# A recommender with neighbour attention on one core: the final part in program order, buffers outside the item stage's space, the last rows finished at once, indices loaded first

## The chip, the core and the metric

The kernel runs on one core of a Trainium2 chip. The metric is device microseconds of one execution. TensorE is called PE, VectorE DVE, ScalarE ACT, GpSimd POOL and SyncE SP, as in the profile.

## What is computed

```python
def neighbour_attention(E, near):                 # 50,001 items, 32 neighbours each
    V = E[near]
    w = softmax(einsum('nd,nkd->nk', E, V) / sqrt(32))
    return einsum('nk,nkd->nd', w, V)
a_sus, a_inf = neighbour_attention(E_in, near), neighbour_attention(E_out, near)
h = concat(E_hist[history], a_sus[history], a_inf[history])    # 128 wide
t = concat(E_tgt[target], a_inf[target], a_sus[target])
z = relu((h * t) @ W1.T + b1)                                  # 128 hidden units
score = z @ W2[0]                                              # one per history entry
```

There are 16384 users with 100 history entries and one target each. The scores of a user go through an exponential, entries equal to the target or to item 0 drop out, and the weighted rows are compared with the target row; a norm over all users enters into the last step, after which a sigmoid gives one number per user.

## The kernel before, in words

**Item stage.** The 50,001 items lie in 23 tiles of 128 partitions x 17 items (`NITER`, `NSUB`). A sub-tile is one item per partition, and two sub-tiles are a batch (`M = 2`), so there are 391 sub-tiles in 196 batches; the last batch has one. `load` (L124 to L129, on SP) brings a tile's neighbour indices `nidx`, its own embeddings `own`, and the first 64 columns of its result `row`. `gather` (L144, on POOL) issues 64 indirect DMAs per batch, each of which fetches one neighbour row for 128 items. `products` multiplies them by the items' own rows (L157 on ACT, L159 on DVE), reduces to scores (L166), and takes the exponentials (L176, ACT). `attended` weights the rows and sums them (L192, L200) and writes the two attention results into `row` (L203). `finish` works once per tile: ACT copies 32 columns (L217), DVE makes the row sum in column 0 (L218), and ACT issues two writes into tables in DRAM: `ttab` (L219, the target's layout) and `table` (L222, 129 columns, for the history). For the last tile it works twice, on 16 rows and on the last one. In the loop over batches `gather(b)` comes first, then `attended(b - 2)`, `products(b - 1)` and `finish(b - 3)`. Engines take their instructions in the order of this code, with waits on semaphores between them; DVE, ACT and SP are in manual schedule here.

The first 64 columns of `ttab` are copied from the target embedding (L109, L110, 12.5 MB, issued by ACT before the loop). The weights `b1`, `w2`, `w1` are loaded on SP before the first tile (L86 to L90), and `w1T` and `pick` are set up from them (L93 to L99).

**User stage.** 128 columns of 128 users; a column has 25 steps of 4 history entries. Per column there is one gather of target rows (L270) and then four gathers of history rows per step (L306), all on POOL; `hidx` are the history indices (L266, SP, four columns a load), `tidx` the target's (L246). PE turns the rows (L320), DVE multiplies them by the turned target (`xT`, L325) and copies the row sums (`hsum`, L328), PE makes the hidden layer (L337), ACT the relu (L339), PE the scores into a bank (L345). `LAG = 3` steps lie between these. There are 20 buffers of rows (`HBUF`). At the end of a column ACT copies the bank (L351), PE turns it (L358), ACT takes exponentials (L360), and DVE sums (L367 to L370). `target_work` (L282 to L293) makes the turned target `tT`, its sum `tsum`, its sum of squares `tsq` (ACT, L288) and the mask `keep`.

**Final part.** `root` is the square root of `den` (L406), `part` and its sum follow on DVE, PE adds over partitions (L413), and DVE and ACT make the norm `n1`, the targets' norms `n2` from `tsq` (L422 the maximum, L423 the square root), `pred` and the sigmoid `res` (L430), which SP writes out (L431). Its tiles are in a pool `f_s` of its own, opened after the pools of the user stage are closed, and the part is not in manual schedule; where its instructions land in an engine's order is the scheduler's choice.

The pools decide who waits for whom beyond the data: `u_in` (history indices), `u_t`, `u_h` (row buffers) are opened after the item stage's pools are closed and take over their space.

Of the kernel before, what the change touches and what calls it, by code (L numbers as in the profile page):

```python
# [53 lines left out]
def kernel(  # L54
# [31 lines left out]
    nc.sync.dma_start(b1_sb, b1.rearrange("(h o) -> h o", o=1))  # L86
# [6 lines left out]
    nc.vector.memset(pick, 0.0)  # L93
    for g in range(NG):
        nc.vector.tensor_copy(pick[:, g, g : g + 1], w2_sb)
    with tc.tile_pool(name="wps", bufs=1, space=bass.MemoryType.PSUM) as wps:
        w1_ps = wps.tile([D, HID], F32, name="w1_ps")
        nc.tensor.transpose(w1_ps, w1_sb, ident)
        nc.vector.tensor_copy(w1T, w1_ps)  # L99


    scale = 1.0 / math.sqrt(G)
    near_v = near.rearrange("(i p j) k -> i p j k", p=P, j=NSUB)
# [6 lines left out]
    nc.scalar.dma_start(ttab[ITEMS - 1 : ITEMS, 0:DE], etgt[ITEMS - 1 : ITEMS, :])  # L110
    with (
        tc.manual_schedule(engines={E.Activation, E.DVE, E.SP}),
        tc.tile_pool(name="n_in", bufs=2) as n_in,
# [21 lines left out]
        def gather(b):  # L135
            v = n_v.tile([P, M, K, 2, G], F32, name="v")
            subs[b]["v"] = v
            for m, s in enumerate(subs[b]["tiles"]):
                it, j = divmod(s, NSUB)
                if j == NSUB // 2 and it + 1 < NITER:  # L140
                    load(it + 1)
                nidx = its[it][0]
                for k in range(K):
                    nc.gpsimd.indirect_dma_start(  # L144
                        out=v[:, m, k].rearrange("p t d -> p (t d)"),
                        out_offset=None,
                        in_=egeo,
                        in_offset=bass.IndirectOffsetOnAxis(ap=nidx[:, j, k : k + 1], axis=0),
                    )
# [60 lines left out]
        def finish(b):  # L210
            for s in subs.pop(b)["tiles"]:
                it, j = divmod(s, NSUB)
                row = its[it][2]
                if j == NSUB - 1 or (it == NITER - 1 and j == NSUB - 2):
                    j0 = NSUB - 1 if it == NITER - 1 and j == NSUB - 1 else 0
                    js = slice(j0, j + 1)
                    nc.scalar.copy(row[:, js, W : W + G], row[:, js, 1 + DE : 1 + DE + G])  # L217
                    nc.vector.tensor_reduce(row[:, js, 0], row[:, js, 1:W], AX.X, ALU.add)  # L218
                    nc.scalar.dma_start(  # L219
                        ttab_v[it][:, js, DE:D], row[:, js, 1 + DE + G : W + G]  # L220
                    )
                    nc.scalar.dma_start(table_v[it][:, js, :], row[:, js, 0:W])  # L222
                if j == NSUB - 1:
                    del its[it]
# [1 line left out]
        NT = NITER * NSUB  # L226
        batches = [range(s, min(s + M, NT)) for s in range(0, NT, M)]
        load(0)
        for b in range(len(batches) + 3):
            if b < len(batches):  # L230
                subs[b] = {"tiles": batches[b]}
                gather(b)
            if 0 <= b - 2 < len(batches):
# [6 lines left out]
    num = const.tile([P, UC], F32, name="num")  # L240
    den = const.tile([P, UC], F32, name="den")
    tsum = const.tile([P, UC], F32, name="tsum")
    tsq = const.tile([P, UC], F32, name="tsq")
    hist_v = history.rearrange("(p i j) l -> i p j l", p=P, j=BSUB)
    tidx = const.tile([P, UC], I32, name="tidx")
    nc.scalar.dma_start(tidx, target.rearrange("(p c) -> p c", p=P))  # L246
    tidf = const.tile([P, UC], F32, name="tidf")
    nc.vector.tensor_copy(tidf, tidx)
    with (
        tc.manual_schedule(engines={E.PE, E.Activation, E.DVE, E.SP, E.Pool}),  # L250
        tc.tile_pool(name="u_in", bufs=4) as u_in,
        tc.tile_pool(name="u_t", bufs=3) as u_t,
        tc.tile_pool(name="u_h", bufs=HBUF) as u_h,
        tc.tile_pool(name="u_x", bufs=6) as u_x,
        tc.tile_pool(name="u_z", bufs=6) as u_z,
        tc.tile_pool(name="u_s", bufs=3) as u_s,
# [4 lines left out]
        users, hists = {}, {}  # L261
        rows, got, hT, xT, z = {}, {}, {}, {}, {}

        def history_of(i):
            hists[i] = u_in.tile([P, BSUB, L], I32, name="hidx")
            nc.sync.dma_start(hists[i], hist_v[i])  # L266

        def target_rows(c):
            t = u_t.tile([P, D], F32, name="t")
# [100 lines left out]
            nc.vector.tensor_reduce(num[:, c : c + 1], ea, AX.X, ALU.add)  # L370

        last = UC * NG
        history_of(0)
        history_of(1)
        target_rows(0)
        target_work(0)
        for s in range(last + 2 * LAG + 6):
# [21 lines left out]
                ended(done)  # L399

    with (
        tc.tile_pool(name="f_s", bufs=1) as f_s,
        tc.tile_pool(name="f_p", bufs=1, space=bass.MemoryType.PSUM) as f_p,
    ):
        root = f_s.tile([P, UC], F32, name="root")
        nc.scalar.activation(root, den, AF.Sqrt)  # L406
        part = f_s.tile([P, UC], F32, name="part")
        nc.vector.reciprocal(root, root)
        nc.vector.tensor_tensor(part, num, root, ALU.mult)
        psum1 = f_s.tile([P, 1], F32, name="psum1")  # L410
# [3 lines left out]
        s = f_s.tile([P, 1], F32, name="s")  # L414
        nc.vector.tensor_copy(s, s_ps)
        n1 = f_s.tile([P, 1], F32, name="n1")

        nc.vector.tensor_tensor(n1, s, s, ALU.mult)
        nc.vector.tensor_scalar(n1, n1, float(D), EPS * EPS, ALU.mult, ALU.max)
        nc.scalar.activation(n1, n1, AF.Sqrt)  # L420
        n2 = f_s.tile([P, UC], F32, name="n2")
        nc.vector.tensor_scalar(n2, tsq, EPS * EPS, None, ALU.max)  # L422
        nc.scalar.activation(n2, n2, AF.Sqrt)  # L423
        nc.vector.tensor_scalar(n2, n2, n1, None, ALU.mult)
        pred = f_s.tile([P, UC], F32, name="pred")
        nc.vector.tensor_scalar(pred, tsum, s, None, ALU.mult)
        nc.vector.reciprocal(n2, n2)
        nc.vector.tensor_tensor(pred, pred, n2, ALU.mult)
        res = f_s.tile([P, UC], F32, name="res")
# [57 lines left out]
```

## Time and profile before

| | us |
|---|---|
| median of 3 runs | 36254.43 |
| these runs | 36249.81 to 36257.75 |
| the profiled execution's own time | 36158.99 |
| its span, first to last instruction | 36157.2 |
| item stage until the last gather's end | 17498.87 |
| last item gather's end to the first history gather | 32.08 |
| last history gather's end to the end of the span | 63.71 |

POOL is busy for 71% of the span, PE for 28%, DVE for 19%, ACT for 7%. A busy share says little here, since POOL's gathers stand in a row with 0.30 us between them that count as idle. A row of a timeline gives the start, the duration, the engine, the line, the operation with its tiles, and in square brackets the idle time before it and what ended it; a small q behind an engine's name is its queue of DMA issues. A row of waits gives the engine, the tile and line that waited, what for, then the microseconds in total, the count and the longest one. A row of a group gives its count, the busy time, the mean in ns, and the idle time just before its instructions.

### The profile page before, as it was taken

To read this page: it belongs to the slowest core of one execution; us is meant where nothing else is said; L and a number is where in the kernel's file an instruction comes from. 1 tells how busy PE (TensorE), PEld (TensorE's weight loads), DVE (VectorE), ACT (ScalarE), POOL (GpSimd) and SP (SyncE) were. 2 spreads that over 40 slices of the span, in tenths; PEclk is the share of its full clock that TensorE was granted. 3 is DMA by queue.
4 is the path that set the end of the run, shared out by engine and by line. 5 is a ranking of instruction groups with operands and counts; after the bars stand their busy time and mean duration, and the time that the engine had idled before them with its cause. 6 is when DMAs were issued, how large, how long until landed. Compare 5 with 4: busy or idle time off the path is not lost.

```text
span 36157.2 us, 104181 instructions
## 1 busy us (share of the span) xinstructions
PE 9955.5 (28%) x26243; PEld 3219.9 (9%) x26243; DVE 6910.6 (19%) x9965; ACT 2692.6 (7%) x5700; POOL 25713.0 (71%) x25446
## 2 busy tenths in 40 slices
PE   0000000000000000000255555555555555555555
PEld 0000000000000000000011111111111111111111
DVE  2222222222222222222111111111111111111111
ACT  0000000000000000000011111111111111111111
POOL 7777777777777777777666666666666666666666
PEclk9999999999999999999877777777777777777777
DMA  1111111111111111111111111111111111111111
GB/s 42 29 27 27 27 28 29 27 27 27 28 29 28 27 27 28 27 29 25 40 47 47 47 47 47 47 46 47 47 47 47 46 47 46 47 47 47 46 46 43
DMA packets 1027956, 1362.32 MB, mean 38 GB/s; under 512 B 559904, under 2 KB 614432, under 8 KB 1027360
## 3 DMA queue, kind: packets, MB, share of 16 engines
q0 software_dynamic: 814080, 1265.42, 14.4%
q10 hardware_dynamic: 151056, 51.51, 0.8%
q1 hardware_dynamic: 62224, 38.72, 0.4%
q8 instruction: 218, 3.57, 0.0%
q14 instruction: 378, 3.10, 0.0%
HBM read 1315.31 MB, written 51.50 MB: 38 GB/s over the span
## 4 chain that ended last, share of the span: by engine, by line
POOL 37%; another core or an unknown queue 29%; PE 18%; issue 13%; DVE 2%; ACT 1%; DMA 0%; POOLq 0%; SPq 0%; ACTq 0%; DVEq 0%
POOL v L144 37%; PE z_ps L337 7%; PE bank L345 6%; PE hT_ps L320 5%; DVE xT L325 1%; ACT z L339 1%; DVE hsum L328 0%; DMA v<-in_egeo_dram,nidx 0%; PE hT_ps L358 0%; POOL h L306 0%; PE hT_ps L282 0%; ACT flat L351 0%; DVE tT L284 0%; DVE keep L293 0%
## 5 line engine op out<-in xcount | busy, mean ns | idle before, releaser
L306 POOL DMA_INDIRECT h<-table,hidx x12800 | 12107.2, 946 | 6300.4 <-issue 3830.4
L144 POOL DMA_INDIRECT v<-in_egeo_dram,nidx x12512 | 13484.1, 1078 | 4013.5 <-issue 3964.1
L325 DVE TENSOR_TENSOR xT<-hT_ps,tT 128x512 f32<-128x512 f32 x3200 | 2198.7, 690 | 15477.9 <-remote 9681.0
L282 PE MATMUL hT_ps<-ident,t 128*128 128x128 f32 x128 | 46.3, 362 | 17780.0 <-DMA t<-ttab,tidx 17522.1
L337 PE MATMUL z_ps<-xT,w1T 128*128 128x512 f32 x6400 | 4177.9, 741 | 1833.5 <-ACT z L339 1463.2
L320 PE MATMUL hT_ps<-ident,h 128*128 128x128 f32 x12800 | 2520.1, 328 | 5521.0 <-DVE xT L325 3984.9
L345 PE MATMUL bank<-z,pick 128*25 128x512 f32 x6400 | 3978.8, 709 | 0.0
L339 ACT ACTIVATE z<-z_ps,b_sb 128x512 f32<-128x512 f32 x3200 | 2149.8, 687 | 15996.4 <-remote 7924.9
L159 DVE TENSOR_TENSOR prod<-v,own_ps 128x4096 f32<-128x4096 f32 x196 | 864.4, 4410 | 12916.3 <-DMA v<-in_egeo_dram,nidx 12850.6
L320 PEld LDWEIGHTS hT_ps<-ident,h 128*128 128x128 f32 x12800 | 1621.4, 163 | 8660.4 <-DVE xT L325 4994.7
L282 PEld LDWEIGHTS hT_ps<-ident,t 128*128 128x128 f32 x128 | 19.1, 149 | 17919.3 <-issue 17586.5
L176 ACT ACTIVATE ex<-sc,top 128x32 f32<-128x32 f32 x782 | 227.8, 291 | 16993.6 <-DVE top L170 12332.7
L192 DVE TENSOR_TENSOR wv<-v,ex 128x1024 f32<-128x1024 f32 x782 | 1378.3, 1875 | 315.9 <-ACT ex L176 299.5
L337 PEld LDWEIGHTS z_ps<-xT,w1T 128*128 128x128 f32 x6400 | 1175.1, 230 | 2056.4 <-ACT z L339 1647.9
L166 DVE TENSOR_REDUCE sc<-prod 128x128 f32<-128x4096 f32 x196 | 864.4, 4410 | 6.7
L200 DVE TENSOR_REDUCE att<-wv 128x128 f32<-128x4096 f32 x196 | 864.1, 4409 | 6.0
L345 PEld LDWEIGHTS bank<-z,pick 128*25 128x25 f32 x6400 | 433.4, 109 | 3095.3 <-issue 3095.3
L328 DVE COPY hsum<-h 128x4 f32<-128x4 f32 x3200 | 568.9, 178 | 0.0
L358 PE MATMUL hT_ps<-ident,flat 25*128 25x25 f32 x512 | 65.8, 249 | 1051.5 <-ACT flat L351 714.5
L270 POOL DMA_INDIRECT t<-ttab,tidx x128 | 121.1, 946 | 65.9 <-issue 64.1
L358 PEld LDWEIGHTS hT_ps<-ident,flat 25*128 25x128 f32 x512 | 51.5, 170 | 1190.1 <-ACT flat L351 777.2
L176 ACT ACTIVATION_READ_ACCUMULATOR ex<-sc,top 128x1 f32 x782 | 146.0, 187 | 0.0
(55 smaller groups left out, 855.7 us busy)
## 6 DMA issues: line engine op xcount, KB each, us to landing
h<-table,hidx POOLq DMA_INDIRECT x12800
v<-in_egeo_dram,nidx POOLq DMA_INDIRECT x12512
table<-row ACTq DMA_DIRECT2D x22, 1096.5 KB
own<-in_egeo_dram SPq DMA_DIRECT2D x23, 544.0 KB
row<-in_ehist_dram SPq DMA_DIRECT2D x23, 544.0 KB
ttab<-in_etgt_dram ACTq DMA_DIRECT2D x1, 12500.0 KB
ttab<-row ACTq DMA_DIRECT2D x22, 544.0 KB
hidx<-in_history_dram SPq DMA_DIRECT2D x32, 200.0 KB
```

What stands on the lines that cost most here:

```text
L144: nc.gpsimd.indirect_dma_start(out=v[:, m, k].rearrange("p t d -> p (t d)"), out_offset=None, in_=egeo, in_offset=bass.IndirectOffsetOnAxi ...
L159: nc.vector.tensor_tensor(prod[:, 0:n].rearrange("p m k t d -> p m k (t d)"), v.rearrange("p m k t d -> p m k (t d)"), own_ps[:, 0:n].to_b ...
L166: nc.vector.tensor_reduce(sc[:, 0:n].rearrange("p m t k -> p m k t"), prod[:, 0:n], AX.X, ALU.add)
L192: nc.vector.tensor_tensor(wv[:, m, t].rearrange("p d k -> p k d"), subs[b]["v"][:, m, :, t, :], ex[:, m, t, :].rearrange("p (k o) -> p k o ...
L200: nc.vector.tensor_reduce(att[:, 0:n], wv[:, 0:n], AX.X, ALU.add)
L306: nc.gpsimd.indirect_dma_start(out=rows[s][:, q, :], out_offset=None, in_=table, in_offset=bass.IndirectOffsetOnAxis(ap=users[c]["hidx"][: ...
L320: nc.tensor.transpose(hT[s][:, q, :], rows[s][:, q, 1:W], ident)
L325: nc.vector.tensor_tensor(xT[s], hT.pop(s), users[c]["tT"].to_broadcast([D, LG, P]), ALU.mult)
L328: copy = nc.vector.tensor_copy(users[c]["hsum"][:, g * LG : (g + 1) * LG], rows.pop(s)[:, :, 0:1].rearrange("p q o -> p (q o)"),)
L337: nc.tensor.matmul(z_ps, w1T, xT.pop(s), start=True, stop=True)
L339: nc.scalar.activation(z[s], z_ps, AF.Relu, bias=b1_sb)
L345: nc.tensor.matmul(users[c]["bank"], pick[:, g, :], z.pop(s), start=g == 0, stop=g == NG - 1)
```

## The change

It has four parts.

1. The weights' loads stand behind the first tile's loads, and so do the target indices and the first two history loads, now on SP. The copy into `ttab`, `tidf`, `pick` and `w1T` are written in batch 1 of the item loop.
2. `finish(b - 2)` stands right behind `attended(b - 2)`; the loop has one turn less. The writes into `ttab` go to SP.
3. The pools of history indices, targets and row buffers are opened before the item stage and have space of their own.
4. The final part is in manual schedule, its tiles are in the pool `const`, and `n2`'s two steps stand behind `root`'s; `s` is called `total`.

The core of the diff:

```diff
-    nc.sync.dma_start(b1_sb, b1.rearrange("(h o) -> h o", o=1))
-    nc.sync.dma_start(w2_sb, w2.rearrange("o h -> h o"))
-    nc.sync.dma_start(w1_sb, w1)
...
-    nc.scalar.dma_start(ttab[0 : ITEMS - 1, 0:DE], etgt[0 : ITEMS - 1, :])
-    nc.scalar.dma_start(ttab[ITEMS - 1 : ITEMS, 0:DE], etgt[ITEMS - 1 : ITEMS, :])
+    u_in = ctx.enter_context(tc.tile_pool(name="u_in", bufs=4))
+    u_t = ctx.enter_context(tc.tile_pool(name="u_t", bufs=3))
+    u_h = ctx.enter_context(tc.tile_pool(name="u_h", bufs=HBUF))
...
-                    nc.scalar.dma_start(
+                    nc.sync.dma_start(
                         ttab_v[it][:, js, DE:D], row[:, js, 1 + DE + G : W + G]
                     )
...
         load(0)
-        for b in range(len(batches) + 3):
+        nc.sync.dma_start(b1_sb, b1.rearrange("(h o) -> h o", o=1))
+        nc.sync.dma_start(w2_sb, w2.rearrange("o h -> h o"))
+        nc.sync.dma_start(w1_sb, w1)
+        nc.sync.dma_start(tidx, target.rearrange("(p c) -> p c", p=P))
+        history_of(0)
+        history_of(1)
+        for b in range(len(batches) + 2):
...
+            if b == 1:
+                nc.scalar.dma_start(ttab[0 : ITEMS - 1, 0:DE], etgt[0 : ITEMS - 1, :])
+                nc.scalar.dma_start(ttab[ITEMS - 1 : ITEMS, 0:DE], etgt[ITEMS - 1 : ITEMS, :])
+                nc.vector.tensor_copy(tidf, tidx)
+                nc.vector.memset(pick, 0.0)
+                for g in range(NG):
+                    nc.vector.tensor_copy(pick[:, g, g : g + 1], w2_sb)
...
             if 0 <= b - 2 < len(batches):
                 attended(b - 2)
+                finish(b - 2)
             if 0 <= b - 1 < len(batches):
                 products(b - 1)
-            if 0 <= b - 3:
-                finish(b - 3)
...
     with (
-        tc.tile_pool(name="f_s", bufs=1) as f_s,
+        tc.manual_schedule(engines={E.PE, E.Activation, E.DVE, E.SP, E.Pool}),
...
         nc.scalar.activation(root, den, AF.Sqrt)
+        nc.vector.tensor_scalar(n2, tsq, EPS * EPS, None, ALU.max)
+        nc.scalar.activation(n2, n2, AF.Sqrt)
```

SP's queue at the start, before: the three weights, then the tiles.

```order
L86 DMA b_sb<-in_b_dram 128x1
L88 DMA w_sb<-in_w_dram 128x1
L90 DMA w_sb<-in_w_dram 128x128
L124 DMA nidx<-in_near_dram 128x544
L126 DMA own<-in_egeo_dram 128x1088
L129 DMA row<-in_ehist_dram 128x17x64
```

The same queue now:

```order
L135 DMA nidx<-in_near_dram 128x544
L137 DMA own<-in_egeo_dram 128x1088
L140 DMA row<-in_ehist_dram 128x17x64
L240 DMA b_sb<-in_b_dram 128x1
L241 DMA w_sb<-in_w_dram 128x1
L242 DMA w_sb<-in_w_dram 128x128
L243 DMA tidx<-in_target_dram 128x128
L120 DMA hidx<-in_history_dram 128x400 x2
```

The first tile's three loads went to the front; the target indices (ACT's before) and two histories stand behind the weights. ACT's order still begins with the copy into `ttab`, as it did.

ACT at the end of the item stage, before; `row` is the last tile's, the last `own_ps` and `ex` are those of the batch with one sub-tile.

```order
L157 COPY own_ps<-own 128x64
L176 ACTIVATE ex,tot<-sc,top 128x32 x2
L217 COPY row<-row 128x16x32
L219 DMA ttab<-row 128x16x64
L222 DMA table<-row 128x16x129
L217 COPY row<-row 128x32
L219 DMA ttab<-row 128x64
L222 DMA table<-row 128x129
```

The same place now, in the new line numbers:

```order
L228 COPY row<-row 128x16x32
L233 DMA table<-row 128x16x129
L168 COPY own_ps<-own 128x64
L187 ACTIVATE ex,tot<-sc,top 128x32 x2
L228 COPY row<-row 128x32
L233 DMA table<-row 128x129
```

The 16 rows of the last tile and their write went ahead of the last batch; the last row's stay behind it, and both writes into `ttab` are on SP. On DVE the reduction of the 16 rows moved ahead of the last batch's `prod` in the same way.

DVE near the end of the user stage, before; `n_79611` is `n2`, and some 20 steps of `xT` and `hsum` follow.

```order
L325 TENSOR_TENSOR xT<-hT_ps,tT 128x512
L328 COPY hsum<-h 128x4
L422 TENSOR_SCALAR n_79611<-tsq 128x128
L325 TENSOR_TENSOR xT<-hT_ps,tT 128x512
L328 COPY hsum<-h 128x4
```

And now, where `n_82` is `n2`; the rows behind it are the last column's `target_work`.

```order
L338 COPY hsum<-h 128x4
L414 TENSOR_SCALAR n_82<-tsq 128x128
L294 COPY tT<-hT_ps 128x128
L296 TENSOR_REDUCE tsum<-t 128x1
L301 CAST idf<-hidx 128x100
L302 TENSOR_SCALAR keep<-idf 128x100
L303 SCALAR_TENSOR_TENSOR keep<-idf,tidf,keep 128x100
```

The maximum of `n2` stood ahead of the last 20 steps and stands now ahead of the last column's target work, so it is still not in the place that the code has for it. Before it waits for all the gathers' semaphores, now for ACT's alone. Its square root on ACT, before between two exponentials' loads of tables in the last steps, now stands behind that of `root`.

More of the change, by code (lines that the diff above doesn't have):

```diff
@@ L107, with history_of @@
     ttab_v = ttab.rearrange("(i p j) d -> i p j d", p=P, j=NSUB)
-    nc.scalar.dma_start(ttab[0 : ITEMS - 1, 0:DE], etgt[0 : ITEMS - 1, :])
-    nc.scalar.dma_start(ttab[ITEMS - 1 : ITEMS, 0:DE], etgt[ITEMS - 1 : ITEMS, :])
+    num = const.tile([P, UC], F32, name="num")
+    den = const.tile([P, UC], F32, name="den")
+    tsum = const.tile([P, UC], F32, name="tsum")
+    tsq = const.tile([P, UC], F32, name="tsq")
+    tidx = const.tile([P, UC], I32, name="tidx")
+    tidf = const.tile([P, UC], F32, name="tidf")
+    root = const.tile([P, UC], F32, name="root")
+    part = const.tile([P, UC], F32, name="part")
+    n2 = const.tile([P, UC], F32, name="n2")
+    pred = const.tile([P, UC], F32, name="pred")
+    res = const.tile([P, UC], F32, name="res")
+    psum1 = const.tile([P, 1], F32, name="psum1")
+    total = const.tile([P, 1], F32, name="total")
+    n1 = const.tile([P, 1], F32, name="n1")
+    hist_v = history.rearrange("(p i j) l -> i p j l", p=P, j=BSUB)
+    u_in = ctx.enter_context(tc.tile_pool(name="u_in", bufs=4))
+    u_t = ctx.enter_context(tc.tile_pool(name="u_t", bufs=3))
+    u_h = ctx.enter_context(tc.tile_pool(name="u_h", bufs=HBUF))
+    hists = {}
+    def history_of(i):
+        hists[i] = u_in.tile([P, BSUB, L], I32, name="hidx")
+        nc.sync.dma_start(hists[i], hist_v[i])
     with (
@@ L260 @@
     ):
-        users, hists = {}, {}
+        users = {}
         rows, got, hT, xT, z = {}, {}, {}, {}, {}
-        def history_of(i):
-            hists[i] = u_in.tile([P, BSUB, L], I32, name="hidx")
-            nc.sync.dma_start(hists[i], hist_v[i])
         def target_rows(c):
@@ L372 @@
         last = UC * NG
-        history_of(0)
-        history_of(1)
         target_rows(0)
```

38 lines of the change are left out of this document (6 added, 32 removed).

## The prediction, made before the changed kernel ran

> **What bounds the kernel now.** I read the page's span and groups first, then the busy time by stretches, then the waits, then the timeline at the start, at the seam of the two stages, and at the end.
>
> ```profile
> span 36157.2 us, 104181 instructions
> L306 POOL DMA_INDIRECT h<-table,hidx x12800 | 12107.2, 946 | 6300.4 <-issue 3830.4
> L144 POOL DMA_INDIRECT v<-in_egeo_dram,nidx x12512 | 13484.1, 1078 | 4013.5 <-issue 3964.1
> ```
>
> POOL issues 25,312 gathers; busy time and the idle time just before them are 12107.2 + 6300.4 + 13484.1 + 4013.5 = 35905.3 us, 99.3% of the span. So nearly every microsecond in which POOL could be at its next gather belongs to the time, and what other engines do is hidden as long as it keeps no gather waiting. The next view, four stretches, tells where that rule ends (columns: stretch, its length, busy us and instructions of PE, PEld, DVE, ACT, POOL, then the granted PE clock, DMA share and GB/s).
>
> ```profile
> 0.00:17499.00 17499.00, 0.45 (x1) 0.18 (x1) 4184.15 (x2391) 402.48 (x1974) 13484.75 (x12518) 1.00 0.13 28
> 17499.00:17531.00 32.00, 0.45 (x1) 0.18 (x1) 14.22 (x15) 1.97 (x8) 1.00 (x2) 1.00 0.37 71
> 17531.00:36094.00 18563.00, 9903.51 (x26089) 3202.58 (x26089) 2692.75 (x7505) 2266.59 (x3686) 12227.28 (x12927) 0.72 0.18 47
> 36094.00:36157.00 63.00, 51.15 (x152) 16.93 (x152) 19.47 (x55) 21.54 (x32) 0.00 (x0) 0.88 0.01 3
> ```
>
> Two stretches in which POOL does next to nothing stand out: 32 us at the seam and 63 us at the end. They are 95 us, 0.26% of the span; the start adds 9.31 us before the first gather (below). The change touches these three places. The gathers themselves, 17499 us for 12512 (1.40 us each) and 18563 us for 12927 records (1.436 us each), stay the same in number, size and order.
>
> What holds the gathers of the two long stretches:
>
> ```profile
> DVE prod L159 <- DMA v<-in_egeo_dram,nidx: 12850.6, 195, 67.2
> POOL h L306 <- PE hT_ps L320: 1786.3, 591, 9.9
> SPq L124 <- DMA v<-in_egeo_dram,nidx: 4219.7, 21, 553.3
> ```
>
> In the item stage DVE waits for the gathers, 65.9 us in each batch, so DVE work can grow there unseen. In the user stage POOL also waits for PE, 591 times with 3.02 us on average, because all 20 row buffers are full. That wait is a loop of POOL, PE, DVE and ACT, and it is the one place where a small shift in time could change the pace.
>
> **The change part by part.** The sum is made in the profiled execution, whose own time is 36158.99 us (span 36157.2 and 1.8 around it). It is 95.4 us (0.26%) below the median of the runs shown, 36254.43, and I take differences over to the median unchanged. The rows of before have before's line numbers.
>
> Start:
>
> ```profile
> 0.75 0.39 SPq L86 DMA_DIRECT2D b_sb<-in_b_dram  x1
> 1.44 50.27 ACTq L110 DMA_DIRECT2D ttab<-in_etgt_dram  x1
> 2.24 0.44 SPq L124 DMA_DIRECT2D nidx<-in_near_dram  x1
> 9.31 1.10 POOL L144 DMA_INDIRECT v<-in_egeo_dram,nidx  x1 [8.00 <-DMA nidx<-in_near_dram]
> SPq L129 <- DMA ttab<-in_etgt_dram: 50.7, 1, 50.7
> 1.00:9.00 8.00, 0.45 (x1) 0.18 (x1) 2.19 (x27) 0.00 (x0) 0.29 (x1) 1.00 0.88 239
> ```
>
> The index load is SP's fourth; in the new order it is the first. It can start at 0.75 instead of 2.24, and with the same 7.07 us until the first gather that gives **-1.5 us**. ACT's copy of 12.5 MB still starts as it did, though the code now has it in batch 1: ACT has nothing ahead of it. New beside the index load is the load of `row` (544 KB), which before waited 50.7 us for that copy: 544 KB at the 239 GB/s of the last row are 2.3 us, so the worst is -1.5 + 2.3 = +0.8. The best is about -5: the four history loads at the seam (quoted below), 200 KB each with no copy beside them, were issued from 17528.98 on and POOL went on at 17530.95, 2 us later, where the index load took 7. A rule of the Trainium skill speaks against the new order: its page "DMA: Bandwidth & Descriptors", section "Issuing engines are not separate DMA queues", says that transfers issued by different engines interleave on the same DMA engines, and that several issuers save only issue time. The 7 us here against 2 us there agree with it; by it the index load would share with everything issued beside it, the start would cost up to +0.8 us, and the sum would end 2.3 us higher.
>
> ```profile
> 5.03 1.61 DVE L95 COPY pick<-w_sb 128x1 f32<-128x1 f32 x25 [3.37 <-DMA w_sb<-in_w_dram]
> ```
>
> The set-up steps (`tidf`, `pick`, the transpose of `w1`) now come in batch 1, where DVE has 65.9 us to wait. If that cover failed they would cost the 1.61 us of `pick`'s copies and under 2 us more. On SP, target indices and histories are queued ahead of the second tile's load, and every `ttab` write ahead of the tile load after it. A tile load has 17 x 44.8 = 762 us from the end of one tile's gathers to the end of the next; the `SPq L124` row shows that SP waits up to 553 us in it for buffers. The writes come about two batches (180 us) after a tile's last gather, so what is left is over 500 us: nothing. The 22 early `finish` reductions (about 2.3 us each) take from DVE's 65.9 us, nothing; uncovered they would be 51 us.
>
> Seam:
>
> ```profile
> 17497.77 1.10 POOL L144 DMA_INDIRECT v<-in_egeo_dram,nidx  x1 [0.30 <-issue]
> 17512.42 0.23 DVE L203 TENSOR_TENSOR row<-att,tot 128x64 f32<-128x64 f32 x1
> 17512.56 2.47 DVE L218 TENSOR_REDUCE row<-row 128x16 f32<-128x2048 f32 x2
> 17514.87 0.37 ACTq L222 DMA_DIRECT2D table<-row  x1
> 17515.28 0.22 ACT L217 COPY row<-row 128x32 f32<-128x32 f32 x1 [8.35 <-DVE row L218]
> 17515.53 1.36 ACTq L219 DMA_DIRECT2D ttab<-row  x1
> 17516.93 1.25 ACTq L222 DMA_DIRECT2D table<-row  x1
> 17519.00:17522.00 3.00, 0.00 (x0) 0.00 (x0) 0.00 (x0) 0.00 (x0) 0.00 (x0) 1.00 1.23 149
> 17523.00:17526.00 3.00, 0.00 (x0) 0.00 (x0) 0.00 (x0) 0.00 (x0) 0.00 (x0) 1.00 0.01 3
> 17526.06 0.95 POOL L270 DMA_INDIRECT t<-ttab,tidx  x1 [27.19 <-issue]
> 17528.98 1.27 SPq L266 DMA_DIRECT2D hidx<-in_history_dram  x4
> 17530.95 0.95 POOL L306 DMA_INDIRECT h<-table,hidx  x1 [3.94 <-DMA hidx<-in_history_dram]
> ```
>
> The last arithmetic (L203, until 17512.65) stays where it is: it hangs on the last gather. Behind it before stand the reduction of 16 rows (2.3 of the 2.47 us), a 1.1 MB write, and two small writes issued one after the other until 17518.18. Now the 16 rows are reduced and written a batch earlier, around 17483. Left are one row's copy (0.22) and reduction, until about 17513.0, and the two small writes side by side on SP and ACT, issued by 17514.4. They are 33 and 66 KB, 0.7 us at the 149 GB/s of 17519 to 17522. Traffic ended near 17523, and POOL went on 3.1 us later; I keep these 3.1. The target gather then comes at 17514.4 + 0.7 + 3.1 = 17518.2, 7.9 us sooner. Bounds: 7.9 us from last issue to POOL as before (17522.3, -3.8), and the 2.33 us that a 64 KB load took here from the end of its issue to its reader (17516.7, -9.4):
>
> ```profile
> 51.74 0.60 ACTq L246 DMA_DIRECT2D tidx<-in_target_dram  x1
> 54.67 0.23 DVE L248 CAST tidf<-tidx 128x128 f32<-128x128 int32 x1 [48.03 <-DMA tidx<-in_target_dram]
> ```
>
> The first history gather came 4.89 us after the target gather, because its indices were loaded only then; with indices long there it comes one gather's pace later, 0.95 + 0.30 = 1.25, another -3.64 (bound 0, if its table writes land last). Together **-11.5 us**, bounds -3.8 and -13.0.
>
> End:
>
> ```profile
> 36092.54 0.95 POOL L306 DMA_INDIRECT h<-table,hidx  x1 [0.30 <-issue]
> 36095.17 0.23 DVE L422 TENSOR_SCALAR n<-tsq 128x128 f32<-128x128 f32 x1 [11.67 <-DMA h<-table,hidx]
> 36096.05 1.12 PE L320 MATMUL hT_ps<-ident,h 128*128 128x128 f32 x4 [6.33 <-DVE xT L325]
> 36100.63 1.12 PE L320 MATMUL hT_ps<-ident,h 128*128 128x128 f32 x4
> 36103.63 0.66 PE L320 MATMUL hT_ps<-ident,h 128*128 128x128 f32 x4
> 36106.05 0.66 PE L320 MATMUL hT_ps<-ident,h 128*128 128x128 f32 x4
> ```
>
> L422 writes a tile in space that the row buffers leave, so it waits for the last gather, and it sits in DVE's order some 20 steps ahead of the end: DVE stands 11.67 us, PE 6.33 behind it. The next two steps take 4.58 and 3.00 us instead of the 2.42 of all later ones. Without it the burst would have run on: 6.33 + 2.16 + 0.58 = 9.1 us. But PE, DVE and ACT get through the backlog in bursts, and where a burst stands when the gathers end is chance; if the burst starts only with the last gather's end (36093.49 and about 0.6 to PE, against 36096.05), only 2 us are won. I take the middle, **-5.6 us**, bounds -2 and -9.1. In the new order the same step (L414) stands ahead of the last user's `tT` and waits only for ACT's sum of squares; queued behind it on DVE are `tT`, `tsum`, `keep` and that user's first `xT`. Up to 5 us of stall lie under the full row buffers there; if that cover is gone they count. I take 0. In the last chain `pred` leaves its place between two steps on `n1`, and the square root of `n2` comes beside DVE's reciprocal: tenths of a microsecond, counted as 0.
>
> Sum: -1.5 - 11.5 - 5.6 = **-18.6 us**, 36235.8 at the median, 36140.4 for a profiled execution. Bounds of these terms: -5.0 - 13.0 - 9.1 = -27.1, and +0.8 - 3.8 - 2.0 + 5 = 0.
>
> **Rivals.** *The user stage gives part of it back.* After the pause at the seam its first 200 us ran faster than the rest:
>
> ```profile
> 17531.00:17731.00 200.00, 73.78 (x143) 22.38 (x143) 16.70 (x47) 11.07 (x18) 135.10 (x143) 0.68 0.19 49
> ```
>
> 143 gathers at 1.436 are 205.4 us, so 5.4 us were gained there. If that came from the long pause and a short one doesn't bring it, and the end wins only 2: -1.5 - 11.5 + 5.4 - 2.0 = -9.6, 36244.8. For it speaks that POOL waited for full buffers only later; against it, that empty buffers alone would do the same.
>
> *Slower: the loop of the user stage settles at a worse pace.* Its place is L306's wait for `hT_ps` (1786.3 us, 591 times). The stage starts 13 us earlier, with buffers elsewhere, and its rhythm is not fixed:
>
> ```profile
> 19000.00:26000.00 7000.00, 3774.97 (x9909) 1219.61 (x9909) 1024.35 (x2853) 862.79 (x1403) 4613.35 (x4878) 0.72 0.18 47
> 26000.00:35000.00 9000.00, 4799.26 (x12683) 1555.87 (x12684) 1311.44 (x3656) 1103.89 (x1797) 5917.02 (x6256) 0.72 0.18 47
> ```
>
> 1.4350 us per gather in one long stretch and 1.4386 in the next, 0.25%, which is 46.7 us over 18563. Seven waits more of 3.02 us would eat the forecast; 31 more (5% of 591, 94 us) bring it to 36330, over 0.2% slower. For it: the 0.25%. Against it: instructions and waits of a step are the same, and three runs lie within 8 us. The same loop may settle better: 18 waits fewer (54 us) give 36181, over 0.2% faster.
>
> *The change doesn't do what it says.* The copy stays at the start, `n2` isn't at the end, and the seam may hang on something that the writes only accompany. Then -3.8 at the seam and +0.8 at the start give 36251.4. By the rule quoted above the start would come out so.
>
> **How the numbers follow.** Forecast 0.58, given back 0.22, no effect 0.06, slower pace 0.07, better pace 0.07. About 0.2% (72.5 us) is what a measurement of this kernel can tell from no change, so only the two cases of pace leave "within 0.2%": faster 0.07, same 0.86, slower 0.07. The range is the forecast with the bounds of its terms (-27.1 to 0) and half the drift of pace (23 us) on either side: 36204 to 36277, cut at 36272 since both upper ends at once are unlikely.
>
> **What the new profile would show.** First gather near 7.8 instead of 9.31; from the last item gather to the first history gather some 20.6 us instead of 32; no wait of DVE for `h` in the last 80 us and no table load of ACT inside the last bursts; last gather to the end about 58 us instead of 63.7; POOL's waits for `hT_ps` near 590 and 1.436 us per gather. I'm wrong if that pace moves by over 0.1%, since it weighs more than all three places, or if the seam shrinks by less than 4 us.

## The result and the profile after

The changed kernel takes 36247.4 us in the median of 14 runs (36226.82 to 36271.7), the kernel before 36258.68 in 14 runs beside them (36249.81 to 36274.07): 11.3 us less, a ratio of 0.9997 with a 95% interval of 0.9989 to 1.0005. The interval holds 1, so this comparison alone doesn't tell a gain from none. It is within 0.2%, the case with the chance 0.86. The forecast was 18.6 us less.

The profiled execution is now the longer one, a span of 36231.5 us against 36157.2, and this misleads. The profile before was taken in an execution of 36158.99 us, 91 us below the lowest of the 14 runs (36249.81); the profile after is one of its 14 runs (36233.66). In later groups of runs the same kernel before took between 31895 and 36288 us (below). The two profiles must be compared place by place, not by their ends.

The start and the seam of the profile after, first to last as in the rows of before:

```profile
...
0.75 0.38 SPq L135 DMA_DIRECT2D nidx<-in_near_dram  x1
...
1.46 51.39 ACTq L252 DMA_DIRECT2D ttab<-in_etgt_dram  x1
1.66 0.64 SPq L140 DMA_DIRECT2D row<-in_ehist_dram  x1
...
4.36 1.10 POOL L155 DMA_INDIRECT v<-in_egeo_dram,nidx  x1 [3.05 <-DMA nidx<-in_near_dram]
...
17492.09 0.94 POOL L155 DMA_INDIRECT v<-in_egeo_dram,nidx  x1 [0.30 <-issue]
...
17506.49 0.23 DVE L214 TENSOR_TENSOR row<-att,tot 128x64 f32<-128x64 f32 x1
17506.74 0.22 ACT L228 COPY row<-row 128x32 f32<-128x32 f32 x1 [6.24 <-DVE row L214]
17506.75 0.29 DVE L229 TENSOR_REDUCE row<-row 128x1 f32<-128x128 f32 x1
17506.99 0.33 SPq L230 DMA_DIRECT2D ttab<-row  x1
17507.06 0.34 ACTq L233 DMA_DIRECT2D table<-row  x1
17509.32 0.94 POOL L280 DMA_INDIRECT t<-ttab,tidx  x1 [16.29 <-issue]
17510.57 0.94 POOL L316 DMA_INDIRECT h<-table,hidx  x1 [0.30 <-issue]
```

The first gather starts at 4.36 instead of 9.31: 3.6 us after the start of the index load's issue, not 7. The two last writes are issued in a third of a microsecond each, not in 1.3, and the target gather follows 1.9 us after them, not 3.8 or 7.9. From the last item gather's end (17493.03) to the first history gather it is 17.54 us instead of 32.08. All in all the first history gather stands at 17510.57, 20.4 us earlier. The stretches after it, in the columns of the four stretches of before:

```profile
17510.00:36173.00 18663.00, 9944.91 (x26095) 3223.15 (x26096) 2697.23 (x7511) 2265.11 (x3688) 12198.88 (x12928) 0.72 0.18 46
36173.00:36231.00 58.00, 47.89 (x149) 15.19 (x148) 18.56 (x52) 19.06 (x30) 0.00 (x0) 0.94 0.01 3
```

The user stage is 100 us longer in this profile than in that of before, which is more than the 20.4 us gained. The experiments had to tell how much of this belongs to the change. The beginning of the stage already showed something (view: stretch of the first 200 us):

```profile
17510.50:17710.50 200.00, 67.33 (x124) 20.42 (x125) 15.23 (x44) 10.09 (x18) 128.87 (x134) 0.64 0.18 44
```

134 gathers now, 143 before: nine gathers, 13 us, are lost in this stretch. What the engines do there (timeline of after, POOL's own rows left out):

```profile
17567.80 1.11 PE L330 MATMUL hT_ps<-ident,h 128*128 128x128 f32 x4 [6.60 <-issue]
...
17607.00 1.12 PE L330 MATMUL hT_ps<-ident,h 128*128 128x128 f32 x4 [12.20 <-issue]
...
17612.55 0.69 ACT L349 ACTIVATE z<-z_ps,b_sb 128x512 f32<-128x512 f32 x1 [21.71 <-remote]
...
17613.29 2.07 PE L347 MATMUL z_ps<-xT,w1T 128*128 128x512 f32 x2 [5.17 <-issue]
...
17615.30 1.90 PE L355 MATMUL bank<-z,pick 128*25 128x512 f32 x2
...
17628.65 0.69 DVE L335 TENSOR_TENSOR xT<-hT_ps,tT 128x512 f32<-128x512 f32 x1 [21.63 <-remote]
```

The rows must be paired by counting steps, since PE runs some steps ahead. The `xT` at 17628.65 is that of step 8 (counted from 0). The turn that it reads ended at 17568.92 (first row), 59.7 us earlier, and a semaphore of PE is all that this `xT` waits for; the turn at 17607.00 is that of step 10. So the news of PE's finished work reaches DVE late, and ACT too, while PE takes up what DVE and ACT finish within a microsecond: its turn at 17607.00 starts right behind an `xT` of 17606.25. One step takes 22.4 us so, while POOL issues one step in 5. When its 20 buffers are full POOL has to wait. Counted over the first 75 steps of this profile, the lag of `xT` behind its turn grows to 65 us by step 9, is down to 0.6 us at step 15, once POOL has waited, and then grows and falls again, up to 39 us. While it is near 0 a step takes some 2.4 us.

### The profile page after: what moved, and what is told of

Its sections match the earlier page's. It is cut to its first block, busy times and chain, and to the rows that moved or that the text cites. A ratio compares the mean times of both kernels' runs of the same rounds, so it can differ in the third digit from the quotient of the medians.

```text
span 36231.5 us, 104145 instructions
## 1 busy us (share of the span) xinstructions
PE 9993.2 (28%) x26243; PEld 3238.5 (9%) x26243; DVE 6913.8 (19%) x9965; ACT 2690.8 (7%) x5698; POOL 25673.9 (71%) x25446
## 3 DMA queue, kind: packets, MB, share of 16 engines
q0 software_dynamic: 814080, 1265.42, 14.5%
## 4 chain that ended last, share of the span: by engine, by line
POOL 37%; another core or an unknown queue 29%; PE 18%; issue 13%; DVE 2%; ACT 1%; DMA 1%; POOLq 0%; ACTq 0%
POOL v L155 37%; PE z_ps L347 7%; PE bank L355 6%; PE hT_ps L330 5%; DVE xT L335 1%; ACT z L349 1%; DMA v<-in_egeo_dram,nidx 1%; DVE hsum L338 0%; PE hT_ps L368 0%; PE hT_ps L292 0%; POOL h L316 0%; ACT flat L361 0%; DVE keep L303 0%; DVE tT L294 0%
```

## Experiments

Two theories went against each other; the first expectation defines them as GIVE-BACK and KEPT. The groups of runs met different conditions. The record gives a chip's number for e1 to e12, and the number 2 stands beside a group of 31898 us and one of 36174 us, so the number doesn't explain them; what does stays open. e5 to e11 are called the quick groups here. Each difference below is against the kernel before, or another kernel, in the same group, unless another group is named.

| group | chip on record | kernel before, median us | one history gather, us |
|---|---|---|---|
| first comparison | not given | 36258.68 | 1.458 |
| e1 to e4 | 12 | 36263.56 | 1.458 |
| e5 to e8 | 2 | 31898.39 | 1.261 |
| e9 to e11 | 1 | 31897.42 | 1.261 |
| e12 | 2 | 36174.18 | 1.451 |

The last column is the time in the group's profiles from the first history gather to the last, by 12799, with the target gathers among them. The first profile of before has 1.450 there, as e12's group and unlike the comparison's own 1.458. The diffs of e3, e4, e10 and e11 are against the changed kernel, those of e5, e6 and e7 against the kernel before.

**e1, the kernel before once more.** 

> The kernel before, unchanged, profiled once more. Two theories stand against each other for the whole study. GIVE-BACK: the shorter pause of POOL at the seam is lost again in the first 500 history gathers, so that only start and end are won. KEPT: the seam's gain stays, and what is missing of it comes from a slower pace of the whole user stage (other places of the buffers, other waits). Both expect here: first gather at 9.3 us, from the last item gather's end to the first history gather 32 us, and the 500th history gather about 715 us after the first. GIVE-BACK expects the pace of the user stage to wander by a few tenths of a per cent from one execution to the next, so 18560 to 18660 us from the first to the last history gather; KEPT expects 18560 again, as in the first profile of this kernel.

One run: 36266.1 us. First gather at 9.66, seam 32.31, 18658.7 us from the first history gather to the last where the first profile had 18561.6 and the changed kernel's 18661.1; e12's has 18573.5. So the 0.54% by which the two first profiles differ isn't the change's.

**e2, the changed kernel once more.** 

> The changed kernel, unchanged. GIVE-BACK: 10 us faster than before (start 5, end 5); first history gather about 17 us behind the last item gather; the 500th history gather about 737 us after the first, 22 more than in the kernel before. KEPT: 25 us faster by the three local gains, less what the pace takes; the 500th history gather 715 us after the first, as before.

36244.25 against 36263.56, 19.3 less, ratio 0.9995 (0.9986 to 1.0004). Seam 17.65 us. The table below has its first gathers: GIVE-BACK expected a loss of 22 us at the 500th gather, and a third of it was there, 7 to 9 us against e1 and e3; at the 120th it is 12 in both profiles with the short pause.

**e3, start and end changed, seam undone.** 

> The changed kernel with its seam undone: history indices, target and row buffers in the item stage's space again, finish late again, target table writes on ACT again, histories loaded in the user stage. Start and final part as changed. GIVE-BACK: the same time as the changed kernel within 4 us, 10 us faster than before; the pause at the seam is 32 us again and the 500th history gather comes 715 us after the first. KEPT: 5 us faster by the start and 5 by the end than before if the pace is before's, and 15 to 20 us slower than the changed kernel if the pace is the same in both.

```diff
-    u_h = ctx.enter_context(tc.tile_pool(name="u_h", bufs=HBUF))
...
+        tc.tile_pool(name="u_h", bufs=HBUF) as u_h,
...
-                    nc.sync.dma_start(
+                    nc.scalar.dma_start(
                         ttab_v[it][:, js, DE:D], row[:, js, 1 + DE + G : W + G]
...
-                finish(b - 2)
...
+            if 0 <= b - 3:
+                finish(b - 3)
```

36245.46: 18.1 less than before, 1.2 more than the changed kernel, whose seam is 14.5 us shorter (32.14 against 17.65). KEPT wanted 15 to 20. The means are 2.7 apart, and by the spread of the 11 runs on either side some 8 us more or less are possible (95%); so KEPT's figure is missed, and in this group the seam shows no gain.

**e4, a pause added.** 

> The changed kernel with 40 memsets on POOL between the first target gather and the first history gather, which lengthen its pause at the seam by an estimated 12 us (0.3 each); nothing else changes. GIVE-BACK: the time is that of the changed kernel within 4 us, since the first 500 history gathers get shorter by what the pause takes (about 725 us instead of 737). KEPT: slower than the changed kernel by those 12 us.

```diff
         target_rows(0)
+        for _ in range(40):
+            nc.gpsimd.memset(idle, 0.0)
         target_work(0)
```

The memsets took 20 us, not 12: the seam is 37.24. The time is 36257.24, 13.0 more than e2, with runs from 36237 to 36275. GIVE-BACK's 4 us are missed, and KEPT's full price of 19.6 lies at the edge of what this spread allows (the means are 11.8 apart, 7 more or less at 95%), so the time alone doesn't settle how much came back. The gathers show the repayment more sharply than the time (us from the first history gather, numbers from 0, from the traces):

```
kernel              pause   xT 7    gather 120   gather 500   gather 2000
before (profile 1)  32.1    69.3    152.6        715.3        2891.7
e12                 32.1    72.1    152.3        715.7        2898.6
e1                  32.3    73.8    152.3        722.8        2910.1
e3                  32.1    72.3    152.3        720.8        2911.7
after (profile 1)   17.5    95.7    164.0        737.3        2920.9
e2                  17.7    95.9    164.2        729.5        2927.0
e4                  37.2    67.0    153.3        722.5        2906.8
e5                  30.0    42.9    152.3        630.5        2521.8
e9                  17.6    43.4    152.7        630.8        2522.5
e8                  76.8    43.9    153.3        631.4        2522.9
```

In the upper seven, a pause of 17.6 us means that the eighth `xT` comes 22 to 27 us later, about one slow step, and gather 120 comes some 11.8 us later than after a pause of 32. With 5 us of pause more than 32, gather 120 gains nothing more; it has nothing left to gain, as some 152 us are also what the lower three rows take. There the pause changes nothing: `xT` starts 0.04 us behind its turn in the median step of e9, 0.6 us at most, whatever the pause was. In the upper seven the first `xT` that is over 0.3 us late is that of step 3 after a pause of 17.6, of step 5 or 6 after one of 32 or 37. e4 has the changed kernel's buffers and queues and a long pause, so at gather 120 it is the pause that decides, not the place of the buffers. From gather 500 on the rows wander by as much as they differ.

**e5, the start alone.** 

> The kernel before with the start alone changed: the first tile's loads ahead of the three weights, and the set-up of w1T and pick in batch 1. Everything after it as before. Both theories: first gather at 4.3 us instead of 9.3 to 9.7, and the 5 us stay, so 5 us faster than before; the seam is 32 us and the 500th history gather comes 715 to 723 us after the first.

```diff
-    nc.sync.dma_start(b1_sb, b1.rearrange("(h o) -> h o", o=1))
...
         load(0)
+        nc.sync.dma_start(b1_sb, b1.rearrange("(h o) -> h o", o=1))
```

31892.52 against 31898.39, 5.9 less (ratio 0.9998, 0.9989 to 1.0007; the interval holds 1, but no run of either kernel lies among the other's), first gather at 4.25: the 5 us are kept. The 500th gather came at 630, not 715, since the user stage runs without the slow steps in the quick groups. The views that tell such a group are POOL's and DVE's waits in e9 (changed kernel), and then DVE's in the first profile of the changed kernel:

```profile
POOL h L316 <- issue: 3590.4, 11780, 0.7
POOL h L316 <- PE bank L355: 151.5, 497, 0.3
POOL h L316 <- PE hT_ps L330: 103.0, 338, 0.3
```

```profile
DVE xT L335 <- PE hT_ps L330: 13102.5, 3165, 6.2
```

```profile
DVE xT L335 <- remote: 9754.0, 814, 31.5
DVE xT L335 <- PE hT_ps L330: 2331.3, 939, 21.7
```

In e9 none of these waits of POOL is over 0.7 us, and DVE waits for PE's turn in 3165 of 3200 steps, never over 6.2 us. POOL alone bounds the user stage there.

**e6, the final part alone.** 

> The kernel before with the final part alone changed (in program order, tiles in the constant pool). Prediction on record: 5.6 us faster, between 2 and 9.1. Rival from the traces so far: the end is as long as the number of steps that are left when the gathers end, 54 us with 16, 59 with 17, 64 to 65 with 18, 68 to 69 with 20, in the kernel before as in the changed one, so that the removed wait of DVE is worth nearly nothing (0 to 2 us) and the shorter end of the changed kernel's profile was chance.

```diff
     with (
-        tc.tile_pool(name="f_s", bufs=1) as f_s,
+        tc.manual_schedule(engines={E.PE, E.Activation, E.DVE, E.SP, E.Pool}),
...
         nc.scalar.activation(root, den, AF.Sqrt)
+        nc.vector.tensor_scalar(n2, tsq, EPS * EPS, None, ALU.max)
+        nc.scalar.activation(n2, n2, AF.Sqrt)
```

31859.06 against 31898.39, 39.3 less (0.9988, 0.9979 to 0.9997), far beyond the prediction and the rival. The reason stands in e5, which has the old final part, where the gathers end (timeline of e5):

```profile
31827.96 0.94 POOL L305 DMA_INDIRECT h<-table,hidx  x1 [0.30 <-issue]
31830.67 0.23 DVE L421 TENSOR_SCALAR n<-tsq 128x128 f32<-128x128 f32 x1 [88.76 <-DMA h<-table,hidx]
31830.81 0.68 DVE L324 TENSOR_TENSOR xT<-hT_ps,tT 128x512 f32<-128x512 f32 x1
31831.55 1.11 PE L319 MATMUL hT_ps<-ident,h 128*128 128x128 f32 x4 [78.68 <-DVE xT L324]
```

DVE stands 88.76 us in front of the maximum of `n2`, and 18 steps pile up that had been free to go. In e6 one step is left when the gathers end (one `xT` starts after that), and the span ends 23.40 us later instead of 62.83: 39.4. In the other groups 16 to 20 steps are left with either final part, a backlog that stands there without this wait.

**e7, the seam alone.** 

> The kernel before with the seam alone changed: pools of history indices, targets and row buffers ahead of the item stage, finish right behind attended, target table writes on SP, target indices and histories loaded at the start; the weights are loaded first as before and the final part is before's (it then stands at the very end and loads ACT's tables twice more there, some 3 us). GIVE-BACK: within 5 us of before, though the first history gather comes 17.6 us behind the last item gather; the 8th xT comes 96 us after the first history gather instead of 69 to 74, and the 500th gather 730 to 737. KEPT: 12 us or more faster than before.

```diff
+    u_h = ctx.enter_context(tc.tile_pool(name="u_h", bufs=HBUF))
...
+        history_of(0)
+        history_of(1)
...
                 attended(b - 2)
+                finish(b - 2)
```

31817.55, 80.8 less (0.9975, 0.9965 to 0.9985), far more than the 5 us of GIVE-BACK and than the 12 that KEPT named as its least. Against e5 the pause is 17.64 instead of 29.99 (-12.4), and nothing of it is given back; the item stage is 15623.6 instead of 15656.1 (-32.6); the end is 24.4 instead of 62.8 (-38.5), since with the row buffers in space of their own the old final part no longer waits for gathers. GIVE-BACK's theory has nothing to act on here.

**e8, a long pause.** 

> The changed kernel with 160 memsets on POOL between the first target gather and the first history gather, a pause of about 97 us in place of 17.6, 79 more. GIVE-BACK, if what a pause stores up is full after some 35 us: the 8th xT comes 65 us after the first history gather as with the 37 us pause, 10 to 15 us are paid back, and the kernel is 65 to 69 us slower than the changed one. GIVE-BACK without such a limit: the 8th xT comes at its unhindered 42 us and steps go on so for some 40 more, and the kernel is less than 40 us slower. KEPT: 79 us slower, nothing paid back.

The edit is e4's with 160 in place of 40. The memsets took 59 us, not 79 (pause 76.8). 31872.63, 25.8 less than before; the changed kernel in the next group (e9) is 87.2 less. So 59.2 us of pause cost 61.4: nothing is paid back where there is no backlog. What 77 us would do in the other groups stays untried.

**e9, the changed kernel in a quick group.** 

> The changed kernel, unchanged, once more. On a chip where the user stage's gathers follow each other at 1.26 us (as in the four runs before this one, where the kernel before takes 31898 us), both theories expect the parts to add up: start 6, seam with its effect on item stage and end 81, and two table loads fewer at the end 3, so 87 to 90 us faster than before; nothing is given back there, since xT follows its gather at once. On a chip where the gathers follow at 1.44 us (36260 us before): GIVE-BACK 10 to 20 us faster, KEPT 25 or more.

31810.26 against 31897.42, 87.2 less, ratio 0.9973 (0.9962 to 0.9983). As both theories expected here, start and seam add up: 5.9 + 80.8 = 86.7. The 39.3 of e6 don't come on top, as the seam alone removes the same wait (e7's end, -38.5).

**e10, target table writes back on ACT; e11, finish late again.** 

> The changed kernel with the writes of the target table issued by ACT again, behind which the big write of the history table stands; all else as changed. If the 32 us that the item stage gained in the last four runs come from the two queues, most of them are lost: on the chip with 1.26 us per gather some 30 us slower than the changed kernel, and POOL waits once per tile for 2.5 us as before. If they come from the early finish, the same time within 5 us. In both cases the seam gets 1 to 2 us longer. On the chip with 1.44 us per gather no more than 4 us between the two.

```diff
-                    nc.sync.dma_start(
+                    nc.scalar.dma_start(
```

> The changed kernel with finish late again (behind the products of the next batch but one, as before); target table writes stay on SP, buffers and index loads as changed. If the item stage's 32 us come from the early finish, they are lost here, and the seam gets some 7 us longer by the 16 rows' reduction and the 1.1 MB write: on the chip with 1.26 us per gather 35 to 40 us slower than the changed kernel. If they come from the two queues, only the 7 us are lost. On the chip with 1.44 us per gather: the pause at the seam grows by 7, of which GIVE-BACK expects most to be paid back (the same time within 5 us), KEPT 7 us slower.

```diff
                 attended(b - 2)
-                finish(b - 2)
...
+            if 0 <= b - 3:
+                finish(b - 3)
```

e10 takes 31844.35, 34.1 more than e9, as its case of the two queues had it; e11 31876.94, 66.7 more. The item stage is 15625.0 us in e9, 15654.8 in e10, 15680.5 in e11, and 15656.1 in e5, which has both undone. The wait that carries it is POOL's for older gathers to land (POOL's waits in e9, e10, e11):

```profile
POOL v L155 <- DMA v<-in_egeo_dram,nidx: 52.4, 154, 1.9
```

```profile
POOL v L155 <- DMA v<-in_egeo_dram,nidx: 86.4, 160, 2.5
```

```profile
POOL v L155 <- DMA v<-in_egeo_dram,nidx: 110.8, 156, 4.6
```

52.4, 86.4 and 110.8 us: 34 and 58 more, which is the difference of the item stages within 5 us. Most of these waits are POOL's usual 0.3 us; over 0.45 us are 10 in e9, 24 in e10 and 22 in e11. The long ones come behind a tile's writes: nearly all in the first three sub-tiles of the next tile with finish early, in the fifth and sixth with finish late. Neither edit does it alone: early finish with both writes on ACT gives the old stage, SP with late finish a worse one (e11's loss is beyond what either case of its expectation named), and only both together win 30 us. Why the order of two transfers decides it, no run shows. The seam of e11 is 28.28, 10.7 more; e10's is the same as e9's, where 1 to 2 more were expected.

**e12, the final part alone, outside the quick groups.** 

> The kernel before with the final part alone changed, once more, since its first run met a chip with 1.26 us per gather, where it was 39 us faster. If this chip does 1.44 us per gather (the kernel before at 36260): the prediction on record expects 5.6 us faster, between 2 and 9.1; the rival, that a backlog of 16 to 20 steps stands at the end with or without DVE's wait, expects 0 to 2; the difference between the kernel with seam undone (16 to 18 faster than before) and its start (5) speaks for 10. If it does 1.26 us per gather: 39 us again, the end of the span 23 to 25 us behind the last gather instead of 63.

36166.8 against 36174.18, 7.4 less (0.9999, 0.9990 to 1.0008), means 4.5 apart; the span ends 58.00 us behind the last gather, with 17 steps left. By the spread of the runs the difference of the means is uncertain by 8 us (95%), so this fits the 5.6 on record and the rival's 0 to 2 alike. DVE still stands about as long as in before (11.67 us) when the gathers end, though the wait of `n2` is gone:

```profile
36107.87 0.69 DVE L333 TENSOR_TENSOR xT<-hT_ps,tT 128x512 f32<-128x512 f32 x1 [11.95 <-PE z_ps L345]
```

## Why the prediction came out right, step by step

**The bound** was read rightly: POOL's gathers, and three places beside them (the four figures add up to 35905.2 us, not 35905.3). The mechanism was right in part only. The sum came out near because the start was taken too small and the seam too large, which is luck; and "within 0.2%" says little, since every rival but those of pace lay in it. For the groups outside the quick ones:

- **Start**, -1.5 forecast, about -5 measured (first gather 9.31 to 4.36; -5.9 in e5, in a quick group). The step that failed is "the same 7.07 us until the first gather". It held the cost of what stood in front: from the index load's issue to the first gather it is 3.6 us now, near the lower bound of -5. That ACT's copy still starts as it did was right (1.46 against 1.44). By the rule of the Trainium skill (page "DMA: Bandwidth & Descriptors", section "Issuing engines are not separate DMA queues") the index load would share with the `row` load and that copy, which the prediction put at up to 2.3 us, an estimate; no such cost shows in the 3.6 us.
- **Seam**, -11.5 forecast. The pause itself shrank by 14.5, a little more than the bound of 13; one reason is that the two writes were issued in 0.33 us each where I took 1.36 from a row in which a bulk write was under way. But in the user stage at least much of it was lost. The step that failed is that the sum counts the seam in full and takes the quicker first 200 us after the long pause for something that "empty buffers alone would do". The rival, at 0.22, had 5.4 us of it given back. The table of e4 shows 11.8 us lost by gather 120 in each profile with the short pause, and e3 is only 1.2 us slower without the seam.
- **End**, -5.6 forecast. The wait was taken as a cost of its own, and outside the quick groups the runs don't show that. The time from the last gather to the end goes by the steps that are left, with the old final part (63.7 us with 18 in before, 69.4 with 20 in e1) as with the new one (54.2 with 16 in e2, 58.9 with 17 in after, 64.5 with 18 in e4, 67.6 with 20 in e3). The profile's -4.8 is one step less. Whether the change leaves fewer steps is open: five profiles with it have 17, 16, 20, 18 and 17 left, two without it 18 and 20, and e12's time allows the forecast as well as nothing.
- **The new wait of `n2`** was as forecast, 0 to 5 us and hidden (view of the one instruction, after):

```profile
L414 DVE TENSOR_SCALAR n<-tsq x1: 382/382/382, 36076.1 to 36076.1; 128x128 f32<-128x128 f32 x1
its engine sat idle before it (us, times) until:
  ACT junk L298: 1.6, 1
```

- **The early finish and the set-up** cost nothing, right. That finish early, with the `ttab` writes on SP, could win something in the item stage was not seen: some 3 to 4 us in the group of e1 to e4, by one profile each (17490.1 and 17489.0 us with it in e2 and e4, 17493.3 without it in e1 and e3; but 17489.6 without it in the first profile of before), and some 30 in the quick groups.

The two comparisons measured -11.3 and -19.3, one near the rival that gives back at the seam and wins 2 at the end (-9.6), one near the forecast (-18.6), so the total doesn't choose between them; e3 and gather 120 speak for the rival. The start alone is -5 of it; how the rest divides between item stage, seam and end stays open. The rival of a slower pace fell: the 0.54% between the first two profiles comes with the group of runs, as e1 and e3, both with before's seam, have the same 18660 us as after.

The largest error shows only in the groups e5 to e11. The forecast took the backlog of the first profile for the kernel's. Where the gathers follow at 1.26 us there is none; then the wait of L422 cost 39 us instead of the 5.6 forecast, the seam's gain is kept, and the same change is 87 us faster (0.27%).

That a pause gives the late news of PE time to reach DVE and ACT is what the rows suggest: in after `xT` lags up to 65 us behind its turn while POOL works, and at the end of POOL's first waits, of 8.6, 16.7 and 5.2 us in front of gathers 120, 124 and 128, the lag is 0.6 us, to grow again some steps later. What holds the news up, and why the quick groups don't show it, stays open; no run tried to take it away.

## What to carry to other kernels

A pause of the bounding engine is worth its length only if nothing downstream uses it: look whether the stage behind it starts slower when the pause is shorter, and count to a fixed item (here gather 120) rather than to the end. An instruction that a scheduler hoists in front of a loop's last steps cost 39 us where these steps had no backlog, and behind a backlog a few us or nothing. And before two profiles are compared by their ends, the kernel before should be profiled in the same group: here its user stage differed by 0.5% and 14% between groups, more than anything that the change did. And a wait must be paired with the work that it waits for by counting, not with the row that stands next to it.

## What was not expected of the hardware

The same program took 36254, 31898 and 36174 us in different groups. In the quick groups the item stage's gathers go at 1.25 us (15625 us for 12512 in e9), in the others at 1.40, and the granted PE clock of the user stage is 0.81 in e9 instead of 0.72 in the first profile:

```profile
4.00:15629.00 15625.00, 0.45 (x1) 0.18 (x1) 4209.86 (x2391) 405.65 (x1975) 11805.02 (x12512) 1.00 0.18 32
15647.00:31786.00 16139.00, 11861.83 (x26212) 3179.45 (x26212) 2749.23 (x7547) 2334.85 (x3706) 12199.34 (x12927) 0.81 0.25 54
```

These are e9's stretches, to be read beside the four of before: POOL's busy time for the item gathers is 11805 instead of 13485 us, and in the user stage it is the same within 0.3% (12199 and 12227). PE has one instruction in the item stage, at a granted clock of 1.00 in both, so its clock can't be what makes the gathers slower there.
